# The way into the second attention of a four-layer graph network: first logits, two counts and a reload moved

## The chip, the cores and the metric

The kernel runs on one core of a Trainium2 chip. The metric is the device time of one execution in microseconds, the median of several runs. The core has TensorE (PE, matrix products), VectorE (DVE), ScalarE (ACT), GpSimd (POOL) and SyncE (SP, which here issues the DMAs). Each works through its own list of instructions in order and waits on semaphores for the others.

## The reference, cut to what matters

Four layers work on 3327 nodes with 256 features: a graph convolution, a graph convolution with a Mamba scan, a graph attention, and a last layer that holds all that is changed here. It takes two steps of diffusion and of attention with a nucleus (top-p) cut:

```
R = (S + I) / rowsum                      # S is the adjacency
Xf = X; Xa = X; Z = 0
for n in range(2):
    q = Xa @ W1.T @ W2.T;  k = Xa @ W3.T
    probs = softmax(q @ k.T)              # 3327 x 3327
    # of each row keep the largest probabilities until their sum passes 0.9
    A = probs * kept;  A = A / A.sum(-1)
    Xf = R @ Xf                           # diffusion
    Xa = A @ Xa                           # attention
    Z = Z + Xf @ U1[n].T + Xa @ U2[n].T
out = layernorm(layernorm(X + Z) + X)     # the inner one with gain g and offset b
```

"The first attention" is the pass n = 0 and "the second attention" the pass n = 1.

## The kernel before, in words

Rows are worked in 26 tiles of 128 (`nt`). For each tile of the second attention these things happen:

- **Logits.** `start(1, t, ...)` (L1655) loads the tile's query `q` by DMA, takes a buffer `e` of 128x3328 numbers, makes the generator `searches[t]` and returns the generator `scores` (L1154 and L1139). That one has four blocks; each is a pair of matmuls of 416 columns into the PSUM tile `sc`, which has one buffer, and a copy on ACT into `e`. The first attention's logits use the same function. The last of the four blocks needs the keys `kT` of tile 25.
- **Search for the cut.** `search_long` (L1421) makes ACT passes over all of `e`: an exp for a root (L1436), the exp proper with its total (L1441), then at a first cut c1 a relu sum (L1456) and a sign sum (L1458), and the same two at a second cut c2 (L1474, L1487). A sign sum is a count of the entries above the cut. Between the passes POOL computes the cuts in small steps (L1444, L1447). DVE then forms c3 (from `x` to L1497), masks each half of `e` to values below c3 (`z`, L1503), takes the top 8 of each segment of 128 (L1353), ranks the candidates in six rounds (L1364, L1366), finds the smallest kept value, drops ties (L1532) and writes the kept weights to `e` (L1540).
- **Weighted sum.** `attended` (L1318) transposes `e` on PE (L1327, 26 squares of 128), copies on ACT (`wt`) and multiplies with the features `G` (L1341), 26 products of 128x256.
- **Diffusion.** `diffused` (L1302) forms on POOL `t` (L1306 and, with `s` loaded from DRAM, L1310), multiplies 26 adjacency squares `at` with the features `F` (L1296, loads of up to five squares into three buffers), and DVE adds the two into `xf` (L1315).
- **End.** `second` (L1586 and on) does two layer norms and the store.

`first` (L1550) closes a tile of the first attention: products with U1 and U2, the sum `s` stored to DRAM (`sd`), the features of the second attention through `g` to DRAM (`gd`), and keys and queries (`store_keys`). The features go by way of DRAM since the place of `G` holds sums of feature blocks until the last pair of tiles is done. Tiles 22 and 23 are closed during the two last, single tiles, 24 and 25, and tile 25 at the end, with nothing beside it. Then `unresolved` checks the first attention's cuts, `G` is reloaded from `gd` by two DMAs (L1786), and the second attention begins.

The order of the second attention is written by hand. A loop (L1798) over i from -2 to 26 takes one step of the generators at a time: `search(i)` of the tile in work, `search(i + 1)` and `search(i + 2)` of the two that follow, the logits of tile i + 2, the weighted sum of tile i - 1 and a share of the diffusion products (`spread`). The iterations -2 to 0 are the way in: they have no weighted sum. Operations wrapped in `here` or `in_order` keep that order; a scheduler places others by their dependencies. POOL's and DVE's small steps are thus placed by the scheduler, and each engine keeps to the list that results.

Of the kernel before, what the change touches and what calls it, by code (L numbers as in the profile page):

```python
# [18 lines left out]
P = 128  # L19
D = 256  # L20
EPS = 1e-5
JH = 13
# [20 lines left out]
DL = 1  # L43
# [7 lines left out]
def gnn_kernel(ctx: ExitStack, tc: tile.TileContext, n: int, a: dict, out: bass.AP):  # L51
    nc = tc.nc
    nt = -(-n // P)
    npad = nt * P
# [122 lines left out]
    with tc.tile_pool(name="l1b", bufs=1) as wpool, tc.tile_pool(name="l1at", bufs=2) as l1at:  # L177
# [3 lines left out]
        with tc.tile_pool(name="l0", bufs=1) as pool, tc.tile_pool(name="l0w", bufs=2) as work, \  # L181
# [11 lines left out]
            for j0 in range(0, nh, J0):  # L193
# [13 lines left out]
                t1, t2, t3, t4 = (x[:, y, :HD] for x in ts)  # L207
# [4 lines left out]
            for i in range(nh):  # L212
                p1, p2, p3, p4, p5, p6, p7 = halved(atp, cmb, psum, i, top, low, ts)
                c = work.tile([P, 2, D + 1], F32, name="c", bufs=1)
                v, u = c[:, 0, HD + 1:], c[:, 1, HD + 1:]
# [9 lines left out]
                for r in range(2):  # L225
                    it = 2 * i + r
# [13 lines left out]
        with tc.tile_pool(name="l1aw", bufs=1) as cwork, tc.tile_pool(name="l1c", bufs=2) as ch, \  # L240
# [70 lines left out]
            ends = []  # L311
# [164 lines left out]
            shares = {}  # L476
# [264 lines left out]
            for k, (c, s) in enumerate(states):  # L741
# [5 lines left out]
                p = plan(c)  # L747
# [97 lines left out]
            h = prods[k % 2]  # L845
# [4 lines left out]
            for i in range(m):  # L850
                it = starts[nch - 1] // P + i
# [14 lines left out]
    half = nt // 2 * P  # L866
    nseg = npad // SEG
    with tc.tile_pool(name="l3", bufs=1) as pool, tc.tile_pool(name="l3d", bufs=1, space=DRAM) as dram:
# [245 lines left out]
        sd, gd = (dram.tile([nt, P, D], F32, name=x) for x in ("sd", "gd"))  # L1114
# [187 lines left out]
        def diffused(work, atp, psum, p, it, out, each=J3):  # L1302

            rd = rdeg[:, it:it + 1]
            t = work.tile([P, D], F32, name="t")
            nc.gpsimd.tensor_scalar(t, (Y if p else X)[:, it, :], rd, None, op0=ALU.mult)  # L1306
            if p:
                s = work.tile([P, D], F32, name="s")
                nc.sync.dma_start(s, sd[it])
                nc.gpsimd.tensor_tensor(t, t, s, op=ALU.add)  # L1310
            for acc in aggregated(atp, psum, it, Y if p else X, each):
                if acc is None:
                    yield
            d = work.tile([P, D], F32, name="xf", bufs=DL + 3)
            nc.vector.scalar_tensor_tensor(d, acc, rd, t, op0=ALU.mult, op1=ALU.add)  # L1315
            out.append(d)

# [61 lines left out]
        def t1(sm, name, w=1):  # L1379
            return sm.tile([P, w], F32, name=name)  # L1380
# [37 lines left out]
        junks = [None]  # L1418
        edge = [None]

        def search_long(work, sm, e, total, v, kept, halves=False):  # L1421

# [1 line left out]

            def t(name):
                return t1(sm, name)

            m8, neg, root = t1(sm, "m8", 8), t1(sm, "neg", 2), t("root")  # L1430
            nc.vector.max(m8, e[:, :KC])
# [19 lines left out]
            c1, nc1 = c1s[:, 0:1], c1s[:, 1:2]  # L1451
            edge[0] = nc.gpsimd.tensor_scalar(lim, total, -TOP_P, None, op0=ALU.mult)
            inverse(rc, c1)
            f1, sg, k1, m1 = t("fs1"), t("sg"), t("k1"), t("m1")
            yield
            here(nc.scalar.activation(junk, e, AF.Relu, bias=nc1, accum_out=f1))  # L1456
            yield
            here(nc.scalar.activation(junk, e, AF.Sign, bias=c1, scale=-1.0, accum_out=sg))  # L1458
            yield
            na, more, room, less, c2s = t("na"), t("more"), t("room"), t("less"), t1(sm, "c2", 2)  # L1460
            scaled(k1, sg, -0.5, npad / 2, ALU.mult, ALU.add)
# [16 lines left out]
            with tc.issue_after(second_cut.ins):  # L1478
# [5 lines left out]
                scaled(big, big, 32.0, HUGE, ALU.is_lt, ALU.mult)  # L1484
                scaled(level, f2, m1, 2.0, ALU.subtract, ALU.mult)
                scaled(level, c2, float(npad), level, ALU.mult, ALU.add)
            here(nc.scalar.activation(junk, e, AF.Sign, bias=c2, scale=-1.0, accum_out=sg))  # L1487
            yield
            x, c3 = t("x"), t("c3")
            nc.vector.reciprocal(s, s)  # L1490
# [59 lines left out]
        def first(work, psum, it, acc, f, xf, tag="pj", xa=None):  # L1550

            xa = work.tile([P, D], F32, name="h") if xa is None else xa
            nc.scalar.mul(xa, acc, f)
            yield
            pt = psum.tile([P, 4, P], F32, name=tag)
            for i, v in enumerate((xf, xa)):
                for k in range(2):
                    tensor.transpose(pt[:, 2 * i + k, :], v[:, k * P:(k + 1) * P], ident)
            xt = work.tile([P, 4, P], F32, name="xt", bufs=1)
            vector.tensor_copy(xt, pt)  # L1560
            yield
            ps = psum.tile([P, 4, P], F32, name=tag).rearrange("p (k x) d -> p k (x d)", k=2)
            for k in range(4):
                tensor.matmul(ps[:, 0, :], xt[:, k, :], (u1 if k < 2 else u2)[:, 0, k % 2, :], start=(k == 0), stop=(k == 3))
            for k in range(2):
                tensor.matmul(ps[:, 1, :], xt[:, k, :], u1[:, 1, k, :], start=(k == 0), stop=(k == 1))
            s = work.tile([P, D], F32, name="s")
            vector.tensor_add(s, ps[:, 0, :], X[:, it, :])
            nc.sync.dma_start(sd[it], s)
            nc.scalar.copy(Y[:, it, :], ps[:, 1, :])  # L1570
            yield
            pg = psum.tile([P, 4, P], F32, name=tag).rearrange("p (k x) d -> p k (x d)", k=2)
            for k in range(2):
                tensor.matmul(pg[:, 0, :], xt[:, 2 + k, :], u2[:, 1, k, :], start=(k == 0), stop=(k == 1))
            project_keys(pg[:, 1, :P], it, xt[:, 2:, :])
            g = G[:, it, :] if tag == "pj" else work.tile([P, D], F32, name="s")
            nc.scalar.copy(g, pg[:, 0, :])
            if tag != "pj":
                nc.sync.dma_start(gd[it], g)
            store_keys(work, pg[:, 1, :P], 1, it)  # L1580
            yield
# [64 lines left out]
        def both(*parts):  # L1646

            parts = list(parts)
            while parts:
                parts = [x for x in parts if next(x, parts) is not parts]  # L1650

        with tc.tile_pool(name="l3w", bufs=2) as work, tc.tile_pool(name="l3s", bufs=4) as sm:


            def start(p, t, es, searches, search):  # L1655
                if p or t:
                    q = work.tile([2 * DA, P], F32, name="q")
                    nc.sync.dma_start(q, qd[p][t])
                else:
                    q = q0  # L1660
                es[t] = work.tile([P, npad], F32, name="e", bufs=4)
                searches[t] = search(work, sm, es[t], *(x[p][:, t:t + 1] for x in (tots, vs, kepts)),
                                     **({"halves": True} if p and t == nt - 1 else {}))
                return scores(work, psum, p, q, es[t])

            with tc.tile_pool(name="l3p", bufs=2, space=PSUM) as psum, tc.tile_pool(name="l3a", bufs=1) as quads:
# [21 lines left out]
                def looks(k):  # L1688
                    for _ in range(k):
                        look()  # L1690
# [24 lines left out]
                def end_pair(i):  # L1715
                    c = next(turned[0])
                    for r in range(2):
                        it = 2 * i + r
                        f = normalizer(sm, kepts[0][:, it:it + 1], tots[0][:, it:it + 1])
                        todo[r] = [first(quads, psum, it, c[:, r, :], f, xfs[it], "tp", c[:, r, :])]  # L1720
                        next(todo[r][0])
                    ends[0] = todo[0][0]
# [16 lines left out]
                for i in range(nh - 1):  # L1739
                    stage(spread, 7, logits(2 * i + 2), ends, counts,  # L1740
                          {0: lambda: end_pair(i - 1) if i else None, 5: lambda: attend_to(i)})
                    counts = [1, 2, 2, 2, 2, 0, 0]
                    queue.append(searches[2 * i + 2])
                    values = turned[0]
                    for k in range(7):
                        next(values)
                        looks(k in (1, 2, 4, 5, 6))
                    stage(spread, 6, logits(2 * i + 3), todo[1], [2, 1, 2, 1, 2, 1], {})
                    finish()
                    queue.append(searches[2 * i + 3])  # L1750
                    for k in range(6):
                        next(values)
                        if k == 0:
                            for _ in spread:
                                pass
                        if k == 3:
                            spread = spreading(i + 2)
                        looks(k > 1)
                end_pair(nh - 2)
                todo = [x for y in todo for x in y]  # L1760
                values = attended(quads, psum, es[nt - 2], X, acc=psum.tile([P, 2, 512], F32, name="acc")[:, 0, :D])
# [2 lines left out]
                for it in (nt - 2, nt - 1):  # L1764
# [14 lines left out]
                        pass  # L1779
                    ends = first(quads, psum, it, acc, f, xfs[it], "tp", c)  # L1780
                    next(ends)
                both(ends)
                fl0 = unresolved(sm, psum, 0)
                fixed = False
            for x in (slice(0, JH), slice(JH, nt)):
                nc.sync.dma_start(G[:, x, :], gd[x].rearrange("t p d -> p t d"))  # L1786

            with tc.tile_pool(name="l3q", bufs=3, space=PSUM) as psum, tc.tile_pool(name="l3at", bufs=3) as atp, \
                    tc.tile_pool(name="l3b", bufs=2) as lone:
                es, searches, xfs = {}, {}, []
                result = iter(())
                spread = (x for j in range(nt) for x in diffused(lone, atp, psum, 1, j, xfs, 1))
                later = (nt - 2) * nt
                shares = [later * (k + 1) // (nt - 1) - later * k // (nt - 1) for k in range(nt - 1)]
                for i in range(-2, nt + 1):  # L1798
                    def search(t):
                        if 0 <= t < nt:  # L1800
                            next(searches[t])
# [3 lines left out]
                        values = attended(lone, psum, es[i - 1], G, 3, in_order(nc.scalar.copy))  # L1805
                    if i + 2 < nt:
                        logits = start(1, i + 2, es, searches, search_long)
                    share = iter(range(shares[i - 1] if 0 < i < nt else nt if -2 < i < 1 else 0))

                    def diffuse(products):  # L1810
                        for _ in range(products):
# [192 lines left out]
```

## Time and profile before

| | |
|---|---|
| runs, median (lowest to highest) | 3408.01 us (3407.56 to 3412.42) |
| profiled execution, own time | 3412.8 us |
| its span | 3411.0 us |
| PE busy | 3129.6 us, 92% |
| DVE busy | 2687.8 us, 79% |
| ACT busy | 1729.9 us, 51% |
| POOL busy | 1132.1 us, 33% |
| mean granted PE clock | 0.965 |
| last matmuls of the first attention | about 2570 us |
| first transposes of the second attention's weights | 2639.46 us |

Times of single instructions are counted from the span's start. A line of a timeline has the start, the duration, engine, line of the code, operation, output and inputs, shape and how often, and in brackets how long the engine had been idle and who released it. A line of the windows view has the stretch, its length, the busy time of PE, PE's weight loads, DVE, ACT and POOL with the number of instructions, the granted PE clock, the share of DMA time and GB/s. A matmul of 32-bit numbers shows as two records.

### The profile page before, as it was taken

Reading aid. Unit: us, or ns where it says so; the run is one execution under the profiler, and the core shown is the slowest. Engines: PE = TensorE matmul, PEld = TensorE weight load, DVE = VectorE, ACT = ScalarE, POOL = GpSimd, SP = SyncE. Lnnn points to the kernel's source line nnn. Section 1 sums busy time; section 2 is a strip of 40 time slices with the busy share of each in tenths; the row PEclk is TensorE's granted clock in tenths of the full one; section 3 lists DMA queues with packets and bytes.
Section 4 is the critical chain, followed back from the end, with each engine's and each line's share of the span. In section 5 each row is a group of like instructions: output and inputs, shape, how many; then the busy total and the mean of one; then the engine's idle time right before and its main releaser. Section 6 shows DMA issues by size and latency. Waiting matters only on the chain. (4 is left out here: it accounts for less than half of the span.)

```text
span 3411.0 us, 50267 instructions
## 1 busy us (share of the span) xinstructions
PE 3129.6 (92%) x18301; PEld 2561.4 (75%) x18301; DVE 2687.8 (79%) x5899; ACT 1729.9 (51%) x2763; POOL 1132.1 (33%) x1328
## 2 busy tenths in 40 slices
PE   8999888988888766999989999999997899999997
PEld 5999656666676555888868888888885677777776
DVE  4665268999999997877578778878863889999996
ACT  1000556767667676111133333333336888888883
POOL 0000145656665654111310000000003566666663
PEclk9999998999999888999989999999998999999999
DMA  6775334434343221544322222323213122222221
GB/s 198 249 254 190 111 99 118 113 109 113 102 122 90 67 59 42 177 139 152 111 88 79 81 72 80 87 65 88 79 49 108 40 68 67 64 63 73 72 63 36
DMA packets 206263, 344.31 MB, mean 101 GB/s; under 512 B 22222, under 2 KB 129166, under 8 KB 205870
## 3 DMA queue, kind: packets, MB, share of 16 engines
q1 hardware_dynamic: 205998, 340.92, 33.8%
q8 instruction: 148, 2.42, 0.3%
q14 instruction: 117, 0.96, 0.1%
HBM read 304.65 MB, written 36.21 MB: 100 GB/s over the span
## 5 line engine op out<-in xcount | busy, mean ns | idle before, releaser
L330 POOL TENSOR_TENSOR h<-du,row 128x2048 f32<-128x2048 f32 (+1 forms) x110 | 465.9, 4236 | 344.6 <-DVE hc L330 249.8
L330 DVE TENSOR_TENSOR_SCAN h<-dA,carry,h 128x512 f32<-128x512 f32 (+1 forms) x384 | 448.9, 1220 | 18.2 <-ACT dA L337 18.1
L337 ACT ACTIVATE dA<-t,A_log 128x512 f32<-128x512 f32 (+1 forms) x448 | 292.6, 658 | 146.9 <-DVE h L330 145.2
L1296 PE MATMUL acc<-F,at 128*128 128x256 f32 x1352 | 343.9, 383 | 3.0 <-DMA at<-in_adjT 2.1
L1341 PE MATMUL acc<-G,wt 128*128 128x256 f32 x1352 | 333.0, 388 | 6.6 <-ACT wt L1139 6.3
L1079 PE MATMUL acc<-F,at 128*128 128x257 f32 x1352 | 303.4, 381 | 0.7 <-ACT r L1023 0.7
L389 PE MATMUL cb<-F,at 128*128 128x256 f32 x1196 | 294.7, 394 | 8.3 <-ACT hn L409 3.4
L1341 PEld LDWEIGHTS acc<-G,wt 128*128 128x128 f32 x1352 | 249.1, 191 | 62.6 <-ACT wt L1139 32.7
L1146 POOL MEMSET e<- 128x1 f32 x52 | 4.9, 99 | 835.2 <-PE tp L891 770.1
L1296 PEld LDWEIGHTS acc<-F,at 128*128 128x128 f32 x1352 | 240.7, 190 | 53.2 <-issue 21.5
L1079 PEld LDWEIGHTS acc<-F,at 128*128 128x128 f32 x1352 | 253.4, 190 | 36.3 <-issue 1.0
L680 PE MATMUL y<-ident,hc 128*128 128x128 f32 x1664 | 235.5, 295 | 46.9 <-DVE hc L330 46.8
L680 PEld LDWEIGHTS y<-ident,hc 128*128 128x128 f32 x1664 | 209.2, 153 | 88.8 <-DVE hc L330 63.9
L389 PEld LDWEIGHTS cb<-F,at 128*128 128x128 f32 x1196 | 229.4, 198 | 58.5 <-issue 19.6
L330 DVE TENSOR_TENSOR hc<-h,row 128x2048 f32<-128x2048 f32 (+2 forms) x114 | 242.9, 2133 | 11.4 <-PE y L680 4.3
L891 PE MATMUL acc<-X,at 128*128 128x128 f32 (+1 forms) x988 | 173.7, 287 | 6.1 <-issue 6.1
L1263 ACT COPY wt<-tp 128x512 f32<-128x512 f32 x156 | 90.8, 589 | 166.1 <-PE tp L891 152.8
L138 PE MATMUL acc<-t,cb 128*128 128x128 f32 (+1 forms) x1014 | 168.4, 275 | 0.0
L891 PEld LDWEIGHTS acc<-X,at 128*128 128x128 f32 x988 | 142.2, 193 | 30.2 <-issue 25.3
L891 PE MATMUL acc<-G,sw 128*128 128x128 f32 x936 | 155.5, 275 | 0.0
L891 DVE MAX8 cand<-e 128x8 f32<-128x128 f32 x676 | 139.8, 277 | 5.5 <-ACT e L1160 3.8
L1160 ACT COPY e<-sc 128x832 f32<-128x832 f32 x78 | 65.9, 845 | 149.4 <-PE sc L891 149.4
(417 smaller groups left out, 7274.2 us busy)
## 6 DMA issues: line engine op xcount, KB each, us to landing
at<-in_adjT SPq DMA_DIRECT2D x54, 832.0 KB, 4.5
at<-in_adjT SPq DMA_DIRECT2D x130, 320.0 KB, 3.0
row<-bc SPq DMA_DIRECT2D x80, 512.0 KB, 5.1
at<-in_adjT SPq DMA_DIRECT2D x52, 640.0 KB, 5.5
at<-in_adjT SPq DMA_DIRECT2D x52, 576.0 KB, 4.3
at<-in_adjT SPq DMA_DIRECT2D x72, 256.0 KB, 3.2
at<-mixed SPq DMA_DIRECT2D x72, 256.0 KB, 3.6
mixed<-cb SPq DMA_DIRECT2D x26, 640.0 KB, 4.2
```

The costliest lines, as they stand in the source:

```text
L138: mm = nc.tensor.matmul(acc, w[:, j, :], x, start=(y == 0 and k % 3 == 0 and k < 6), stop=(y == nh - 1 and k in (2, 6)))
L330: return lambda *x, **k: tc.keep_in_program_order(op(*x, **k))
L337: decays.append(op(*x, **k))
L389: ten.matmul(acc, at[:, j % JC, :], X0[:, j, :], start=(j == 0), stop=(j == nt - 1))
L680: x = ten.matmul(y[:, g * P:(g + 1) * P], h[:, g, i * P:(i + 1) * P], ident, is_transpose=True, start=(first and g == 0), stop=(last and g ...
L891: return lambda *x, **k: tc.keep_in_program_order(op(*x, **k))
L1079: nc.tensor.matmul(acc, at[:, j, :], F[:, j0 + j, :], start=(j0 + j == 0), stop=(j0 + j == nt - 1))
L1146: nc.gpsimd.memset(e[:, n:], NEG)
L1160: copy(halves[:, :, c0:c0 + ws[0]], pl[:, :, :ws[0]])
L1263: nc.scalar.copy(wts[-1], pt)
L1296: nc.tensor.matmul(acc, at[:, j, :], rhs[:, j0 + j, :], start=(j0 + j == 0), stop=(j0 + j == nt - 1))
L1341: tensor.matmul(acc, wt[:, j, :], rhs[:, j0 + j, :], start=(j0 + j == 0), stop=(j0 + j == nt - 1))
```

## The change

- `search_long` gets a function `signs` for the two counts. For tile 0 (`counted`) it takes each count on DVE, as two tensor_scalar instructions over half of `e` each, with a sum and a small step behind, where the others keep ACT's sign pass.
- `start(1, 0)` is called in the first attention's end. The four blocks of tile 0's logits are interleaved with the steps of `first` for tile 25, in the first attention's PSUM pool.
- Tiles 22 to 25 write their features straight into `G`, without `gd`. The reload of `G` covers tiles 0 to 21 and stands ahead of the end of tiles 22 to 25.
- The iterations -2 and -1 of the loop are replaced by a list of pairs: a step of a search (or, with `None`, of tile 1's logits) and a number of diffusion products. In it tile 1's logits and root pass stand beside tile 0's passes. The loop now begins at 0.
- `xf` gets one more buffer (5 instead of 4).

```diff
-            d = work.tile([P, D], F32, name="xf", bufs=DL + 3)
+            d = work.tile([P, D], F32, name="xf", bufs=DL + 4)
...
-        def search_long(work, sm, e, total, v, kept, halves=False):
+        def search_long(work, sm, e, total, v, kept, halves=False, counted=False):
...
+            def signs(c):
+                ks, sg = t1(sm, "ks", 2), t("sg")
+                if counted:
+                    for h in range(2):
+                        z = lone.tile([P, half], F32, name="z", bufs=1)
+                        nc.vector.tensor_scalar(z, e[:, h * half:(h + 1) * half], c, 0.0, op0=ALU.is_gt, op1=ALU.add,
+                                                accum_out=ks[:, h:h + 1])
+                    nc.vector.tensor_add(sg, ks[:, :1], ks[:, 1:])
+                    nc.vector.tensor_scalar(sg, sg, -2.0, float(npad), op0=ALU.mult, op1=ALU.add)
+                else:
+                    here(nc.scalar.activation(junk, e, AF.Sign, bias=c, scale=-1.0, accum_out=sg))
+                return sg
...
-            here(nc.scalar.activation(junk, e, AF.Sign, bias=c1, scale=-1.0, accum_out=sg))
+            sg = signs(c1)
...
-            here(nc.scalar.activation(junk, e, AF.Sign, bias=c2, scale=-1.0, accum_out=sg))
+            sg = signs(c2)
...
-            g = G[:, it, :] if tag == "pj" else work.tile([P, D], F32, name="s")
+            direct = tag == "pj" or it >= nt - 4
+            g = G[:, it, :] if direct else work.tile([P, D], F32, name="s")
             nc.scalar.copy(g, pg[:, 0, :])
-            if tag != "pj":
+            if not direct:
                 nc.sync.dma_start(gd[it], g)
...
-                                     **({"halves": True} if p and t == nt - 1 else {}))
+                                     **({"halves": t == nt - 1, "counted": t == 0} if p else {}))
...
+                for x in (slice(0, JH), slice(JH, nt - 4)):
+                    nc.sync.dma_start(G[:, x, :], gd[x].rearrange("t p d -> p t d"))
                 end_pair(nh - 2)
...
-                both(ends)
+                es, searches = {}, {}
+                groups = start(1, 0, es, searches, search_long)
+                for _ in ends:
+                    next(groups)
+                    next(groups)
+                both(groups)
                 fl0 = unresolved(sm, psum, 0)
                 fixed = False
-            for x in (slice(0, JH), slice(JH, nt)):
-                nc.sync.dma_start(G[:, x, :], gd[x].rearrange("t p d -> p t d"))
...
-                for i in range(-2, nt + 1):
+                groups = start(1, 1, es, searches, search_long)
+                for t, products in ((0, 0), (0, 0), (None, 0), (None, 4), (0, 0), (None, 0), (None, 4),
+                                    (0, 0), (0, 0), (None, 0), (None, 4), (0, 0), (None, 0), (None, 4),
+                                    (0, 0), (1, 0), (1, 4), (0, 0), (0, 6)):
+                    next(groups if t is None else searches[t], None)
+                    for _ in range(products):
+                        next(spread)
+                for i in range(nt + 1):
...
-                    share = iter(range(shares[i - 1] if 0 < i < nt else nt if -2 < i < 1 else 0))
+                    share = iter(range(shares[i - 1] if 0 < i < nt else nt if i < 1 else 0))
```

More of the change, by code (lines that the diff above doesn't have):

```diff
@@ L1453, in search_long @@
             inverse(rc, c1)
-            f1, sg, k1, m1 = t("fs1"), t("sg"), t("k1"), t("m1")
+            f1, k1, m1 = t("fs1"), t("k1"), t("m1")
             yield
@@ L1781, in gnn_kernel @@
                     next(ends)
-                both(ends)
+                es, searches = {}, {}
[4 more added lines that the diff above has]
+                both(groups)
                 fl0 = unresolved(sm, psum, 0)
                 fixed = False
-            for x in (slice(0, JH), slice(JH, nt)):
-                nc.sync.dma_start(G[:, x, :], gd[x].rearrange("t p d -> p t d"))
             with tc.tile_pool(name="l3q", bufs=3, space=PSUM) as psum, tc.tile_pool(name="l3at", bufs=3) as atp, \
                     tc.tile_pool(name="l3b", bufs=2) as lone:
-                es, searches, xfs = {}, {}, []
+                xfs = []
                 result = iter(())
```

## The prediction

> **What bounds the kernel now.** I read the windows view first, to see where TensorE (PE) is not full. From the middle of the second attention on it is full: 50.00 of 50 us, at a granted clock of 1.00. The hole lies at that attention's start.
>
> ```profile
> 2550.00:2575.00 25.00, 20.82 (x102) 15.79 (x100) 2.79 (x9) 5.86 (x15) 1.55 (x4) 0.92 0.17 43
> 2575.00:2600.00 25.00, 22.20 (x83) 13.38 (x84) 1.08 (x2) 18.93 (x18) 4.96 (x12) 0.81 0.53 165
> 2625.00:2650.00 25.00, 15.57 (x72) 11.93 (x73) 22.38 (x65) 14.89 (x13) 11.19 (x24) 0.80 0.16 49
> 2950.00:3000.00 50.00, 50.00 (x246) 38.51 (x245) 45.56 (x136) 45.10 (x44) 32.06 (x66) 1.00 0.26 76
> ```
>
> So whatever PE loses between about 2562 and 2700 us is never caught up, and what it does not lose there comes off the end. PE's timeline shows the loss:
>
> ```profile
> 2570.64 1.48 PE L1154 MATMUL sc<-kT,q 64*128 64x416 f32 x4 [1.93 <-ACT q L907]
> 2573.12 1.76 PE L1154 MATMUL sc<-kT,q 64*128 64x416 f32 x4 [0.99 <-ACT e L1139]
> ...
> 2639.46 1.97 PE L1327 MATMUL tp<-ident,e 128*128 128x128 f32 x8 [9.09 <-DVE e L1540]
> ```
>
> The idle brackets from 2562 to 2640 us add up to 19.0 us. The longest is 9.09 us ahead of the first transposes of tile 0's weights (I call their start T0): PE has run out of products and waits for VectorE (DVE). From T0 to 2702 the brackets give 8.75 us more, mostly DVE's e again. So the start is bound by **tile 0's chain**, logits to T0. The chain of waits in this window, and the timelines of ScalarE (ACT), DVE and GpSimd (POOL), give its joints:
>
> ```profile
> 2592.13 3.06 ACT junk L1456 x2
> ...
> 2595.99 3.07 ACT junk L1458 x2
> ...
> 2604.29 3.17 ACT junk L1474 x2
> 2607.49 3.16 ACT junk L1487 x2
> ```
> ```profile
> 2581.33 3.07 ACT L1436 ACTIVATE junk<-e,neg 128x3328 bf16<-128x3328 f32 x1
> ...
> 2591.28 0.85 ACT L1139 COPY e<-sc 128x832 f32<-128x832 f32 x1 [2.24 <-PE sc L1154]
> ```
> ```profile
> 2610.76 0.27 DVE L1444 TENSOR_SCALAR x<-sg,c,level 128x1 f32<-128x1 f32 x1 [5.20 <-ACT junk L1487]
> ...
> 2612.74 1.95 DVE L1503 SCALAR_TENSOR_TENSOR z<-e,c 128x1664 f32<-128x1664 f32 x1
> ...
> 2628.70 0.16 DVE L1490 RECIPROCAL s<-s 128x1 f32<-128x1 f32 x1 [2.03 <-POOL s L1444]
> ...
> 2635.72 3.67 DVE L1540 SCALAR_TENSOR_TENSOR e<-e,v 128x3328 f32<-128x3328 f32 x1
> ```
> ```profile
> 2579.87 0.72 POOL L1310 TENSOR_TENSOR t<-t,s 128x256 f32<-128x256 f32 x1 [4.21 <-DMA s<-sd]
> ...
> 2617.83 2.57 POOL L1306 TENSOR_SCALAR t<-F,rdeg 128x256 f32<-128x256 f32 x1 [2.10 <-DVE xf L1315]
> ```
>
> The reader is to see four ACT passes of 3.2 us in series with POOL's small steps between (L1456 to L1487), tile 1's logit copies in their midst, and then a DVE stretch of 27 us.
>
> [...] The trace's 128x1664 z row takes 1.95. [...] POOL's t at L1306, usually 0.94 us, took 2.57 beside a z[...]. I take 1.95 us plus 0.08 for the accumulator read[...]. [...] the same four score records take 1.76 us around 2575 and 0.97 later.
>
> **The change, step by step**, on the time scale of the profile before. I use the order of instructions on each queue of the changed program.
>
> *Logits of tile 0.* Before, they start after all of the first attention (2570.64), with PE slow and each block of about 2.7 us (1.76 score, 0.95 wait for the copy); e is whole at 2581.25. After, block 1 stands right behind the last transposes (2563.6) and the others between the projections of tile 25. The projections wait about 0.1 us more. Block 2 runs at 2567.3. ACT's copies of tile 25 (G 0.37, kT 0.26, q 0.26) and of the blocks (0.85 each) interleave; block 4 needs tile 25's keys and block 3's copy, so it runs at 2571.5 to 2572.4; the last two copies (0.9) end at **2573.4: 7.9 us earlier**. [...] I take scores at 0.9.
>
> *Root and exp.* 2573.4 + 3.15 + copy 0.8 + 3.2 = 2580.6; POOL's c1 comes 0.45 later, 2581.05 (before 2588.8). POOL's in-order queue holds t+s, which waits for a load of s, ahead of these small steps. Before it ran at 2579.87, the load having started next to the second reload of G. After, the reload is issued before the last four tiles' stores and s should land near 2575.5: no delay. If it is as late as before, +3.3 us.
>
> *First count.* Before, c1 to c2 took 15.5 us: a 2.24 us wait for logits, copies of 2.6, passes of 3.2 and 3.2, and 5.2 on POOL (1.65 of it two large t operations). After, two DVE halves of 2.03 plus two small ones (0.4) end at 2585.5, beside ACT's relu pass (2581.4 to 2584.6); POOL's steps alone take 3.45 (tile 1's, 2624.11 to 2627.56). **c2 at 2589.0, 15.2 us earlier.**
>
> *Second count.* It ends at 2589.0 + 4.5 = 2593.5, but ACT's relu pass at c2 stands behind the rest of tile 1's copies and its root pass, which starts at 2587.95 and ends at 2591.15: relu 2594.35. On POOL, the two t operations of tile 2 now stand ahead of the two level steps, and t waits for a buffer that DVE's xf of tile 0 frees, itself queued behind the count: 2594.0 + 0.95 + 0.75 + 0.65 = 2596.4. Before, this stretch (c2 to x) took 6.5; after, 7.4. Lead 14.4. With t out of the way it would be 2595.1.
>
> *Candidates.* x to the end of 26 MAX8 is 11.5 us in both: 2607.9. Ranking to the end of e took 17.1 us with a 2.03 us wait for POOL's s of tile 1. That s now comes from ACT's passes on tile 1 (relu 2601.0, sign to 2608.2, root of tile 2 to 2611.5, POOL meanwhile to c2 2611.8, then s at 2613.9); DVE arrives at 2612.8, so the wait is 1.1. **T0 = 2607.9 + 16.2 + 0.1 = 2624.2, 15.2 us earlier** than 2639.46. ACT has finished tile 1's two signs by 2618.2, so nothing there is late for DVE's next tile.
>
> *After T0* the orders agree but for three products (3 x 0.47 = 1.4 us of PE), which lie after T0 now (75 ahead instead of 78). The DVE-bound waits of 8.75 us up to 2702 hide them. Next late is DVE's e of tile 1, as before.
>
> *At nothing:* the four copies that write G directly replace copies of equal length and drop four stores (0.33 us of SP each) and a 1.46 us wait, all beside PE's work; the reload of G has until 2626 to land; the extra xf buffer issues nothing; ACT loses two passes (6.3 us), which are the ones counted above. SP still has q and s loads ahead of adjacency loads: the q for tile 2 waits for tile 0's block 4, now 2572.4 instead of 2579.4, so those come no later.
>
> **Unknowns, both ends.** [...] Late s: 0 to +3.3. PE slow where I took it fast: 0 to +2. Hidden products: 0 to +1.4. Better order at the t operations and no wait for s: down to -2.4. So the gain is 15, from about 6 to about 20.
>
> **Rivals.** *A, the chain as worked out (0.66):* 15 us. *B, half of it (0.22):* the first logits come early, but POOL's t+s or ACT's root of tile 1 takes the place of the removed sign passes; only the 7.9 us of the logits stays, 3400. For it: 4.21 us of waiting on s and ACT at 22 of 25 us at 2600 to 2625. Against: without G's reload there is no cause for the late load. That the change does not do what it says belongs here: if the early query load or tile 25's keys held block 1, only the count would pay, about 6 to 7 us. *C, more (0.08):* PE never slows and the waits after T0 shrink too, 20 us, 3388. Against: tile 1's DVE stretch is not shortened. *D, slower (0.04):* with the hole gone, PE is granted a lower clock in the full stretch. Its place is 2725 to 3350, about 620 us of PE at 1.00: from a clock of 0.976 down the 15 us are used up; at 0.965 it is 3408 + 7 = 3415. Against: the clock row is 9 wherever PE is full; its 8s lie where PE is emptier.
>
> **The numbers.** The profiled execution took 3412.8 us (span 3411.0, 1.8 around it), 4.8 above the median of 3408.01. 3412.8 - 15 = 3397.8; on the median's scale 3393. The range 3385 to 3402 takes in A with its bounds and most of B and C. Faster by over 0.2% (6.8 us, about what a measurement can tell): A, C and most of B, 0.88; within: the rest of B, 0.08; slower: D, 0.04.
>
> **What would show it.** In the profile after: e of tile 0 whole near 2573; count halves of about 1.95 us; c2 near 2589; T0 near 2624 with an idle bracket of about 4 us; 50 of 50 later at 1.00. It is wrong if T0 moves by much more or less than the end does, if the count rows differ from 1.95, or if POOL's t+s still waits near 2580.

## The result, and the profile after

| | before | after |
|---|---|---|
| median of 7 runs each | 3411.88 us (3407.56 to 3418.32) | 3398.83 us (3394.59 to 3401.61) |
| ratio, 95% interval | | 0.9965 [0.9956, 0.9975] |
| span of the profiled execution | 3411.0 us | 3397.0 us |
| A: last transposes of the first attention | 2563.18 us | 2558.14 us |
| T0: first transposes of tile 0's weights | 2639.46 us | 2621.31 us |
| T0 - A | 76.3 us | 63.2 us |
| end - A | 847.8 us | 838.9 us |

The change makes the kernel 0.35% faster: 0.0035 of 3411.88 is 11.9 us, with an interval of 8.5 to 15.0. A is a mark of mine: the last `tp<-ident,sw` row on PE, which belongs to tile 25 in the first attention. Of the change, only the early reload and the direct writes of tiles 22 and 23 work before it, yet it came 5.0 us sooner in this profile. Over all profiles of this study A lies between 2553.6 and 2564.8 us, and e12 (below), which has neither of the two, has it at 2557.45. So the 5.0 of the 14.0 us between the spans are no more than executions differ among themselves, and **end - A, 8.9 us shorter, is the part of this profile that lies behind the change's place**. It is 3 us less than the runs show, but inside their interval. All stages are compared by their distance from A from here on.

The windows view after, for the four stretches shown of before (stretch, length, then busy time of PE, PE's loads, DVE, ACT and POOL, PE clock, DMA share, GB/s):

```profile
2550.00:2575.00 25.00, 20.12 (x97) 14.29 (x97) 2.74 (x7) 13.99 (x20) 4.84 (x9) 0.96 0.21 69
2575.00:2600.00 25.00, 24.53 (x104) 15.96 (x103) 16.43 (x38) 19.84 (x18) 10.56 (x28) 0.97 0.37 108
2625.00:2650.00 25.00, 22.19 (x108) 17.14 (x105) 22.13 (x68) 21.16 (x22) 11.38 (x26) 0.96 0.20 56
2950.00:3000.00 50.00, 50.00 (x245) 37.19 (x244) 45.85 (x140) 42.67 (x44) 31.50 (x57) 1.00 0.21 60
```

PE is full again later, at a clock of 1.00, as before. In the stretch at 2575 it is now busy for 24.53 us at 0.97 instead of 22.20 at 0.81, and DVE has work there (16.43 instead of 1.08 us): the counts.

The joints of tile 0's chain, from ACT's and then DVE's timeline after (start, duration, engine, line, operation, operands, and in brackets the idle time before it and who ended it):

```profile
2568.53 3.07 ACT L1449 ACTIVATE junk<-e,neg 128x3328 bf16<-128x3328 f32 x1
...
2584.11 0.91 ACT L1139 COPY e<-sc 128x416 f32<-128x416 f32 x2 [2.30 <-PE sc L1154]
2585.05 3.07 ACT L1449 ACTIVATE junk<-e,neg 128x3328 bf16<-128x3328 f32 x1
...
2588.30 3.07 ACT L1487 ACTIVATE junk<-e,c 128x3328 bf16<-128x3328 f32 x1
```
```profile
2576.04 1.95 DVE L1435 TENSOR_SCALAR_CACHE_REDUCE z<-e,c 128x1664 f32<-128x1664 f32 x1 [2.98 <-POOL c L1457]
...
2592.29 0.27 DVE L1457 TENSOR_SCALAR x<-sg,c,level 128x1 f32<-128x1 f32 x1 [3.18 <-POOL level L1457]
...
2610.39 0.16 DVE L1503 RECIPROCAL s<-s 128x1 f32<-128x1 f32 x1 [2.12 <-POOL s L1457]
...
2617.56 3.69 DVE L1553 SCALAR_TENSOR_TENSOR e<-e,v 128x3328 f32<-128x3328 f32 x1
```

The first L1449 row is tile 0's root pass; it starts at A + 10.4, and the first count half at A + 17.9. The second L1449 row is tile 1's root pass. It stands between tile 0's second cut (c2 is there by 2584.12, when its count starts) and tile 0's second relu pass (L1487), and tile 1's last logit copies ahead of it waited 2.30 us for PE. That puts L1487 at 2588.30, and DVE's x waits 3.18 us for what POOL makes of it.

PE's timeline after, at its first products, at T0 and at tile 1's transposes:

```profile
2572.17 3.86 PE L1296 MATMUL acc<-F,at 128*128 128x256 f32 x10 [2.70 <-issue]
...
2577.04 2.43 PE L1296 MATMUL acc<-F,at 128*128 128x256 f32 x10
...
2621.31 1.31 PE L1327 MATMUL tp<-ident,e 128*128 128x128 f32 x10 [2.04 <-DVE e L1553]
...
2647.75 1.69 PE L1327 MATMUL tp<-ident,e 128*128 128x128 f32 x8 [2.81 <-DVE e L1553]
2649.23 1.92 PE L1296 MATMUL acc<-F,at 128*128 128x256 f32 x4
```

The bracket at T0 fell from 9.09 to 2.04 us. Ten records of products (five products) took 3.86 us behind the first wait, where the ten that follow take 2.43 us; four records took 1.92 us behind the 2.81 us wait, where the same row took 1.03 in the kernel before. Up to 62.5 us past T0, PE also waited 1.69 and 1.54 us for ACT's copies `wt` and 4.28 us for tile 2's e.

After T0 something is given back: tile 2's e is whole 60.5 us after T0 instead of 56.7, and end - T0 is 775.7 instead of 771.5 us. Two DVE rows carry it, and a POOL row that one of them leads to:

```profile
2652.26 0.48 DVE L1600 SCALAR_TENSOR_TENSOR h<-acc,f,xf 128x256 f32<-128x256 f32 x1 [4.26 <-PE acc L1341]
...
2678.08 0.16 DVE L1503 RECIPROCAL s<-s 128x1 f32<-128x1 f32 x1 [1.65 <-POOL s L1457]
```
```profile
2671.61 0.94 POOL L1306 TENSOR_SCALAR t<-F,rdeg 128x256 f32<-128x256 f32 x1 [5.00 <-DVE xf L1315]
```

The same place in the kernel before, PE and then DVE:

```profile
2665.60 1.06 PE L1327 MATMUL tp<-ident,e 128*128 128x128 f32 x8 [1.19 <-DVE e L1540]
2666.51 1.03 PE L1296 MATMUL acc<-F,at 128*128 128x256 f32 x4
```
```profile
2666.47 0.16 DVE L1490 RECIPROCAL s<-s 128x1 f32<-128x1 f32 x1 [1.01 <-POOL s L1444]
...
2668.44 0.48 DVE L1586 SCALAR_TENSOR_TENSOR h<-acc,f,xf 128x256 f32<-128x256 f32 x1 [1.55 <-PE acc L1341]
...
2692.37 0.15 DVE L1490 RECIPROCAL s<-s 128x1 f32<-128x1 f32 x1
```

Behind tile 1's e, DVE waited 2.56 us in two steps before and 4.26 us after, 1.7 us more. The wait of 1.65 us for POOL's s ahead of tile 2's e did not exist before. Together they are 3.4 of the 3.8 us by which tile 2's e is later.

### The profile page after: what moved, and what is told of

The parts are those of the page before. It is cut to its first block, busy times and chain, and to the rows that moved or that the text cites. A ratio compares the mean times of both kernels' runs of the same rounds, so it can differ in the third digit from the quotient of the medians.

```text
span 3397.0 us, 50257 instructions
## 1 busy us (share of the span) xinstructions
PE 3123.9 (92%) x18301; PEld 2562.3 (75%) x18301; DVE 2697.8 (79%) x5911; ACT 1723.8 (51%) x2759; POOL 1125.4 (33%) x1328
## 5 line engine op out<-in xcount | busy, mean ns | idle before, releaser
L1296 PEld LDWEIGHTS acc<-F,at 128*128 128x128 f32 x1352 | 241.8, 191 | 57.2 <-issue 24.3
L1440 ACT ACTIVATE junk<-e,c 128x3328 bf16<-128x3328 f32 x50 | 154.1, 3082 | 0.0
```

What stands on the lines that cost most here:

```text
L1296: nc.tensor.matmul(acc, at[:, j, :], rhs[:, j0 + j, :], start=(j0 + j == 0), stop=(j0 + j == nt - 1))
L1440: here(nc.scalar.activation(junk, e, AF.Sign, bias=c, scale=-1.0, accum_out=sg))
```

## The experiments

Each kernel was run beside the kernel before on the same chip: e1 to e4 on one, e5 to e8 on a second, e9 to e11 on a third, e12 on a fourth. "PE idle" is the length less PE's busy time in the windows view: first from A to 66 us past T0, then from A to the end.

| | median us | ratio to before, 95% | T0 - A | end - A | PE idle, start | PE idle, all |
|---|---|---|---|---|---|---|
| before | 3411.88 | | 76.3 | 847.8 | 27.6 | 49.8 |
| after | 3398.83 | 0.9965 [0.9956, 0.9975] | 63.2 | 838.9 | 20.8 | 44.1 |
| e1 the changed kernel again | 3399.05 | 0.9967 [0.9954, 0.9980] | 63.3 | 838.7 | 18.8 | 42.0 |
| e2 signs on ACT | 3399.04 | 0.9964 [0.9951, 0.9977] | 66.0 | 838.2 | 20.0 | 42.9 |
| e3 logits late | 3401.47 | 0.9972 [0.9962, 0.9983] | 65.6 | 841.3 | 24.3 | 47.6 |
| e4 reread late | 3399.74 | 0.9961 [0.9944, 0.9977] | 64.6 | 837.9 | 19.5 | 41.6 |
| e5 old order, the rest kept | 3395.33 | 0.9955 [0.9939, 0.9971] | 63.4 | 835.1 | 16.9 | 39.6 |
| e6 nine products in the list's last pair | 3395.58 | 0.9957 [0.9940, 0.9973] | 62.7 | 835.9 | 12.6 | 38.8 |
| e7 third t buffer | 3399.24 | 0.9968 [0.9956, 0.9981] | 62.2 | 838.7 | 18.8 | 42.7 |
| e8 relu first | 3391.38 | 0.9946 [0.9930, 0.9962] | 58.0 | 832.1 | 14.3 | 37.3 |
| e9 logits alone | 3400.97 | 0.9977 [0.9970, 0.9984] | 70.6 | 841.7 | 24.7 | 47.2 |
| e10 logits and reread | 3405.46 | 0.9988 [0.9982, 0.9995] | 72.3 | 845.3 | 26.4 | 49.2 |
| e11 relu first, twelve products in the last pair | 3399.51 | 0.9974 [0.9962, 0.9987] | 60.6 | 840.8 | 15.7 | 43.1 |
| e12 counts alone | 3405.73 | 0.9985 [0.9972, 0.9998] | 70.2 | 844.2 | 25.1 | 47.6 |

PE's busy time from A to the end (end - A less the last column) is 794 to 798 us in all of them. So **the end is PE's work, nearly the same in all, plus PE's idle time, wherever that lies**. "Nearly" counts where effects are small: of the 8.9 us between before and after, 5.8 are idle time and 3.2 are busy time (slow rows, such as the 3.86 us for 2.43 above, count as busy). T0 alone does not give the end: e2 has its T0 2.8 us later than the changed kernel and an end no later.

The profiles of the changed kernel, of e1 and of e7, which have one order, agree within 0.2 us in end - A, though T0 - A differs by up to 1.1 us. The edits also shift how many diffusion products the traces show ahead of T0: 75 in the changed kernel, 78 in e2, 70 in e4, 74 in e5 and e6, 68 in e8. A difference is therefore that of an edit with what the scheduler made of it.

**First round: one part undone at a time.** e1 is the changed kernel. The edits of the others:

```diff
# e2
-    **({"halves": t == nt - 1, "counted": t == 0} if p else {})
+    **({"halves": t == nt - 1, "counted": False} if p else {})
# e3
-                for _ in ends:
-                    next(groups)
-                    next(groups)
+                both(ends)
                 both(groups)
# e4
-            direct = tag == "pj" or it >= nt - 4
+            direct = tag == "pj"
...            # and both rereads of G, over all tiles, behind the first attention
```

> The changed kernel itself, once more. In its first profile the instructions ahead of the last transposes of tile 25 (which the change does not touch) came 5.0 us earlier than in the profile of before; from those transposes to the first transposes of tile 0's weights (T0) it took 63.2 us against 76.3. Theory 'noise ahead': the 5 us are run-to-run variation of the earlier layers; here the transposes of tile 25 lie anywhere within 2558 +- 6 us, the stretch to T0 is again 63.2 +- 0.3 and from T0 to the end 775.7 +- 1.5, and the ratio of times stays at 0.9965 +- 0.001. Rival 'placement': the change makes earlier layers faster; then the transposes stand at 2558 +- 1 again.

> Tile 0's two counts go back to ScalarE's sign passes; all else stays. Theory 'the counts pay because they free ScalarE': two passes of 3.2 us return to its queue, tile 1's passes come 6.4 us later, and VectorE, which waits in tile 0's ranking for a number of tile 1, follows: stretch to T0 63.2 -> 69 to 70 us, time +5 to +6.5 us (+0.15 to 0.19%). Rival 'the logits alone pay': relu and sign fit beside other work and T0 moves by less than 1 us.

> Tile 0's logits are made after tile 25 is closed, no longer between its projections (still ahead of the check of the first attention's cuts); all else stays. Theory: tile 0's root pass, now 10.4 us after the last transposes of tile 25, starts 5 to 8 us later and T0 with it: stretch 63.2 -> 68 to 71 us, time +5 to +8 us. Rival 'ScalarE's queue decides': tile 0's search is held up later in any case, and T0 moves by less than 3 us.

> The features go through DRAM for all tiles again and the second reload stands after the first attention, as before; logits, counts and order of passes stay. Theory: s for GpSimd and the first adjacency squares land behind 1.7 MB of features: GpSimd's t + s 4 to 5 us later, the first cut 1 to 2 us later, and T0 with it: stretch 64.5 to 66.5 us, time +1 to +3.5 us. Rival 'hidden anyway': no change of T0 (within 0.5 us).

Measured: e1 repeated the stretches from A to T0 and to the end. Its A of 2558.53 us suits its rival too; against the rival speaks that A lies at 2564.78 in e6 and at 2557.45 in e12. Each part undone costs 2.4 us at the most, in end - A and in the medians, and by the runs none of the three differs from e1 beyond the intervals. e2 missed widely: T0 came 2.8 us later instead of 6 to 7, and the end was no later, for end - T0 was 772.2 instead of 775.7 us. e3 missed too, as its rival said; it undoes only a part of the logits' lead, since tile 0's root pass starts at A + 13.1, against A + 15.3 in e12, where the logits stand in their old place, and A + 10.4 in the changed kernel. In e4 T0 came 1.4 us later, as expected, but the end did not follow. Two readings were left: the list of the way in brings the rest, or the parts stand in for each other, so that taking one away shows little.

**Second round: the list, and what lies after T0.**

```diff
# e5: the list goes, the loop begins at -2 again
-                groups = start(1, 1, es, searches, search_long)
-                for t, products in ((0, 0), (0, 0), (None, 0), (None, 4), (0, 0), (None, 0), (None, 4), ...
-                for i in range(nt + 1):
+                for i in range(-2, nt + 1):
# e6
-                                    (0, 0), (1, 0), (1, 4), (0, 0), (0, 6)):
+                                    (0, 0), (1, 0), (1, 4), (0, 0), (0, 9)):
# e7, at L1305 and L1601
-            t = work.tile([P, D], F32, name="t")
+            t = work.tile([P, D], F32, name="t", bufs=3)
# e8: tile 0's second relu ahead of tile 1's root pass
-                                    (0, 0), (1, 0), (1, 4), (0, 0), (0, 6)):
+                                    (0, 0), (1, 0), (0, 0), (1, 4), (0, 6)):
```

> Undone: the list of the way in. The loop starts at -2 again, so that tile 1's logits and passes stand where they stood before the change, behind tile 0's; the early logits, the counts on DVE and the early reload stay. Theory (what counts is TensorE's idle time from the first attention's last transposes to 66 us past the second's first ones: 27.5 us before, 20.5 and 18.3 in two profiles of the changed kernel): tile 1 comes late again, the idle time rises to 23 to 26 us and the end, counted from the first attention's last transposes, is 4 to 6 us later than the 838.8 of the changed kernel. Rival (the list only changes who waits; the early logits and the reload bring all of it): within 1.5 us of the changed kernel. Rival from the prediction's sum (the lead at the first transposes decides): with tile 0's chain free of tile 1's passes the first transposes come 1 to 3 us earlier than 63.2, and the end as much earlier.

> Three more products on TensorE just ahead of the first transposes (the list's last pair asks for 9 instead of 6), so that 111 instead of 104 stand ahead of tile 2's. Nothing else is moved ahead of the first transposes. Theory (idle time of TensorE decides, and the lead at the first transposes is given back because too few products lie ahead of tile 2): the first transposes keep 63.2 within 1 us after the first attention's last ones, the waits of TensorE for tiles 1 and 2 shrink from 10.3 us to 7 to 9, and the end comes 1.5 to 4 us earlier. Rival (after the first transposes VectorE's chain decides, and products only fill its waits): end within 1 us. Rival (the three products delay tile 0): first transposes 1.4 us later and the end 1 to 2 us later.

> One more buffer for the features' step t on POOL (3 instead of 2), nothing else: the order of TensorE's and VectorE's instructions is that of the changed kernel. In the changed kernel POOL's t at 2671.61 waits 5.00 us for VectorE's xf, and VectorE's reciprocal at 2678.08 then 1.65 us for POOL. Theory (that wait is a part of what is lost after the first transposes): the 1.65 us goes, the third tile's logits are whole 1.5 to 2 us earlier, and the end with them. Rival (VectorE waits for the products next, whoever released it first): the waits move to h and the end stays within 0.8 us.

> In the list tile 0's second ReLU pass goes ahead of tile 1's root pass (3.07 us each on ACT), the products ahead of the first transposes fall from 75 to 68. Theory (tile 1's root pass, which starts late because TensorE is late with tile 1's scores, stands in tile 0's chain): x of tile 0 comes 2.5 to 3.3 us earlier, the first transposes 2 to 3 us earlier than 63.2 after the first attention's last ones; since seven products are lost ahead of them, tile 1 then waits longer for products or root pass and half or more of that is given back: end 0 to 1.5 us earlier. Rival (lead decides): end 2 to 3 us earlier. Rival (idle time decides): idle time up by 2 to 4 us and the end as much later.

*e5* went against all three theories: without the list the end is 3.8 us **earlier** by the profile, at the same T0 - A. The intervals of e5 and of the changed kernel overlap. But e7, which keeps the list and ended as the changed kernel did, ran beside e5 on the same chip, and in 63 of the 66 pairs of one run of each e5's is the shorter; the medians differ by 3.9 us. So with the other three parts in place the list costs time. Without the counts it is the other way round: e2 has the list and e10 (third round) has not, and their intervals lie apart, at 12.3 and 4.1 us of gain. PE's row for tile 1 in e5:

```profile
2650.28 1.06 PE L1327 MATMUL tp<-ident,e 128*128 128x128 f32 x8 [2.38 <-DVE e L1553]
```

After 2.38 us of waiting the eight transposes took 1.06 us (1.69 in the changed kernel after 2.81), DVE's h waited 2.15 us instead of 4.26, and the wait for POOL's s did not come up. That is 2.1 + 1.65 = 3.8 us, nearly all of the difference in tile 2's e (56.6 against 60.5 us past T0). What in the list brings these waits about is not shown. Nor does a wait of a given length always come with a slow row behind it. Tile 1 of e4, then tile 2 of e8 and tile 2 of e6:

```profile
2653.31 1.45 PE L1327 MATMUL tp<-ident,e 128*128 128x128 f32 x8 [2.04 <-DVE e L1553]
```
```profile
2673.93 1.94 PE L1327 MATMUL tp<-ident,e 128*128 128x128 f32 x8 [2.46 <-DVE e L1553]
```
```profile
2686.30 1.06 PE L1327 MATMUL tp<-ident,e 128*128 128x128 f32 x8 [2.47 <-DVE e L1553]
```

Tile 1 of e8 (shown below) took 1.06 us after 2.05. So a bracket's length alone does not decide it; what does is not shown.

*e6* ended as its theory said, 3.0 us earlier by end - A and with no delay at T0, though its six runs reach from below those of e7 into their upper half, so that the runs do not settle it. The trace has the products elsewhere than expected: 74 stand ahead of T0, one fewer than in the changed kernel, and 111 instead of 104 ahead of tile 2's transposes. There PE's two waits for ACT's `wt` are gone, its wait for tile 2's e is 2.47 instead of 4.28 us, and DVE no longer waits for POOL's s; h of tile 1 still waits 4.26 us. PE's waits in the 62.5 us from T0, without the one at T0, fall from 10.3 to 5.3 us. The lowest idle time at the start (12.6 us) is partly given back later: 5.0 us of idle follow up to the last 350 us, where the changed kernel has 2.9. *e7* refutes its theory: the reciprocal's wait fell from 1.65 to 0.37 us, but another of 1.10 us came up at tile 1's reciprocal, and the end stayed within 0.2 us.

*e8* has the largest gain of all: its six runs (3388.80 to 3395.23) lie below all eleven of e7 (3396.16 to 3407.76), which ran beside it and differs from the changed kernel by a buffer that brought nothing. ACT's, DVE's and PE's rows:

```profile
2583.69 3.08 ACT L1487 ACTIVATE junk<-e,c 128x3328 bf16<-128x3328 f32 x1
...
2586.90 3.07 ACT L1449 ACTIVATE junk<-e,neg 128x3328 bf16<-128x3328 f32 x1
```
```profile
2587.68 0.27 DVE L1457 TENSOR_SCALAR x<-sg,c,level 128x1 f32<-128x1 f32 x1 [0.44 <-POOL level L1457]
```
```profile
2643.63 1.06 PE L1327 MATMUL tp<-ident,e 128*128 128x128 f32 x8 [2.05 <-DVE e L1553]
```

L1487 now stands ahead of L1449, x waits 0.44 instead of 3.18 us and comes 3.3 us earlier (A + 30.8 instead of A + 34.2), and the wait of 2.12 us for tile 1's s is gone from tile 0's chain. T0 is 5.2 us earlier and the end 6.8 us, more than any of the three theories said, so nothing of it was given back. The 3.3 us at x are the pass moved; e8 also has 68 instead of 75 products ahead of T0, and what that adds was not taken apart.

**Third round: parts added one by one to the kernel before,** in the old order, and e8 with more products.

```diff
# e9: e5 with e2's and e4's edits     e10: e5 with e2's edit
# e11: e8 with
-                                    (0, 0), (1, 0), (0, 0), (1, 4), (0, 6)):
+                                    (0, 0), (1, 0), (0, 0), (1, 4), (0, 12)):
# e12: the kernel before with `signs` and
-    **({"halves": True} if p and t == nt - 1 else {})
+    **({"halves": t == nt - 1, "counted": t == 0} if p else {})
```

> The first part of the change alone: tile 0's logits in the first attention's end. Old order of the second attention (loop from -2, tile 1 behind tile 0), signs of tile 0 on ACT, all tiles of gd reread after the first attention. Counted from the first attention's last transposes, the end was 847.8 us before, 838.8 in the changed kernel and 835.1 in the old order with the three other parts (e5). Theory (the parts overlap: each undone alone cost 2.4 us or nothing, the logits 2.4): the logits alone bring 5 to 8 us, end at 840 to 843. Rival (the logits are what the 2.4 us of e3 say, and the counts bring the rest once the list is away): 845 to 846.

> The early logits and the early reread of the features, in the old order, with tile 0's signs on ACT. From e5 it differs by the counts alone, from e9 by the reread alone. Theory (the counts shorten tile 0's chain by 2 x 1.0 us and free 6.2 us of ACT for tile 1; in the old order nothing of tile 1 waits for VectorE instead): end 1.5 to 3.5 us later than e5's 835.1. Rival (as e2 showed in the new order, the counts bring nothing): within 1 us of e5. The reread: TensorE's wait for its features' blocks (10.0 us in e4) is gone against e9, and the end 0 to 2 us earlier.

> e8 (tile 0's second ReLU ahead of tile 1's root pass) with the list's last pair at 12 products instead of 6, so that 67, 89 and 111 products stand ahead of the first transposes of tiles 0, 1 and 2 instead of 68, 87 and 104. Theory (e6's gain of 3 us came from TensorE's waits for tiles 1 and 2, which e8 still has: 0.85 to 2.46 us each, 6.9 in all): first transposes within 1 us of e8's 58.0, end 1.5 to 3.5 us earlier than e8's 832.1. Rival (e8 has taken the same time away already): end within 1 us of e8.

> The kernel before with one part of the change: tile 0's two sign passes as count halves on VectorE. Logits, reread and order as before. Theory (ACT is what tile 0 and tile 1 share: without the two passes of 3.07 us tile 0's second ReLU and tile 1's passes come sooner, worth 10.2 us between e10 and e5): the counts alone bring 7 to 10 us, the end 838 to 841 us after the first attention's last transposes instead of 847.8, the first transposes 7 to 9 us earlier than 76.3. Rival (only tile 0's own chain gets shorter, by two times 3.07 + 0.18 - 3.97): 2 to 3 us. Rival (the counts are worth something only with the early logits): within 1.5 us of the kernel before.

*e9*: the early logits alone bring 7.8 us by the ratio (5.5 to 10.2), as its theory said, though their delay in e3 cost only 2.4. *e10*: the early reread on top did not help but cost 3.6 us in end - A, and 4.5 us between the medians of 22 runs each, taken side by side; the ends of the two intervals just overlap, and e10's run is the longer in 372 of 484 pairs. PE's wait ahead of its first products did fall from 5.80 to 2.15 us, but DVE's wait for tile 1's s grew from 2.25 to 4.41. In the list's order (e4) the reread made no difference. Why it costs in the one order is open.

*e10 to e5* adds only the counts: end - A falls by 10.2 us, far more than expected. ACT's timelines show how, first e10, then e5:

```profile
2582.21 3.09 ACT L1440 ACTIVATE junk<-e,c 128x3328 bf16<-128x3328 f32 x1
...
2585.42 3.07 ACT L1449 ACTIVATE junk<-e,neg 128x3328 bf16<-128x3328 f32 x1
...
2589.00 3.07 ACT L1487 ACTIVATE junk<-e,c 128x3328 bf16<-128x3328 f32 x1 [0.42 <-POOL c L1457]
...
2592.20 3.07 ACT L1440 ACTIVATE junk<-e,c 128x3328 bf16<-128x3328 f32 x1
```
```profile
2587.39 3.07 ACT L1449 ACTIVATE junk<-e,neg 128x3328 bf16<-128x3328 f32 x1
...
2590.64 3.07 ACT L1487 ACTIVATE junk<-e,c 128x3328 bf16<-128x3328 f32 x1
```

The two L1440 passes are gone. Counted from A, L1487 starts 3.5 us sooner (30.2 against 33.7) and x comes 3.7 us sooner; since ACT also gets to tile 1 sooner, DVE's wait of 4.41 us for tile 1's s is gone too. That makes 8.1 of the 8.9 us that T0 gains.

*e12*: the counts alone bring 5.1 us (0.7 to 9.5) by the ratio, between theory and rival, and 3.6 us by end - A. PE's first score blocks in e12, where the code ahead is that of before:

```profile
2566.85 0.97 PE L1154 MATMUL sc<-kT,q 64*128 64x416 f32 x4 [1.00 <-ACT e L1139]
2568.77 0.97 PE L1154 MATMUL sc<-kT,q 64*128 64x416 f32 x4 [0.95 <-ACT e L1139]
```

In the profile of before these rows took 1.76 us. Tile 0's root pass starts at A + 15.3 in e12 and at A + 18.2 before. So 2.9 of the 76.3 us of T0 - A before go with PE's slow rows in that execution; how often they fall there two profiles cannot tell.

*e11* failed: the end is 8.7 us later than in e8. DVE waits 2.77 us for tile 1's s again, T0 is 2.6 us later, PE's bracket there is 5.73 us, and 4.2 us of idle time stand in the last 200 to 60 us, where e8 has 0.9. That the products taken earlier are missing there is likely, but no run shows it.

By the ratios, then: logits 7.8 us, counts 5.1, logits with reread 4.1, the same with the list 12.3, logits with reread and counts 15.3, these three with the list 11.9 and with the list in e8's order 18.4. The counts and the list stand in for each other: on top of logits and reread each brings 8 to 11 us alone, and both together no more than one.

## Why the prediction was right, and where not

It forecast 15 us, 3393.0, and the measurement gives 11.9: inside the range, on the predicted side. By end - A the gain is 8.9 us, so the 15 were too many by 3 to 6 us. A sign that the prediction itself named for being wrong came up: T0 moved by 13.1 us against A, the end by 8.9.

- **Logits.** Predicted 7.9 us; root pass at A + 10.3 predicted, A + 10.4 measured. But 2.9 of the 7.9 were PE's slow rows in the one profile of before, which the prediction showed (1.76 against 0.97) and yet counted as the change's. That the sum came out is in this part luck.
- **First count.** Four halves of 1.95 us were expected, 1.95 with 0.08 for the read were measured; POOL's small steps beside the second count (2584.29 to 2585.85) took 0.19 to 0.31 us each, the same steps before 0.19 to 0.34. c2 at A + 25.8 predicted, A + 26.0 measured. The estimate, drawn from the z row of before (1.95 us for 128x1664, 0.08 for its read), held.
- **Second count.** The mis-sized term. Tile 1's root pass ahead of the relu was seen, but its start was put at 2587.95 on the scale of before, A + 24.8; it was A + 26.9. The rows point to the unknown "PE slow where I took it fast", taken at 0: PE's first products waited 2.70 us and ran at 3.86 for 2.43, so tile 1's scores came late. No run took this alone; the rows only agree with it. x was due at A + 33.2 and came at A + 34.2, although POOL's t was not in the way.
- **Ranking.** The wait for tile 1's s was 2.12 us instead of 1.1. With the second count this makes T0's lead 13.1 instead of 15.2 us.
- **After T0.** The step that failed: "the orders agree but for three products ... hide them". 4.2 us were lost there, 1.7 of them where DVE waited for tile 1's products, behind PE's slow rows after a 2.81 us wait (1.69 us for 1.06, 1.92 for 1.03), and 1.65 at POOL's s. In e5 neither came up, and end - T0 is 771.7 us, where before had 771.5. Taking most of the second away alone brought nothing (e7). The prediction also misread the waits that were to hide the products: of its 8.75 us, 3.63 are DVE's e and 5.12 ACT's `wt`. In the changed kernel the waits up to the same row did not shrink but grew, to 11.2 us against 8.75, so that nothing was hidden; seven more products ahead of tile 2's transposes made them shorter (e6).
- **The reread at nothing.** Right for the changed kernel (e4); as part of the old order it cost (e10).
- The profiled spans differ by 14.0 us, close to the 15, but only because 5.0 us of variation ahead of A fill what was lost after T0. That is luck.
- Rival D is out: 50.00 of 50 us at 1.00. Rival B cannot be put aside. Its 8 us are almost as near to 11.9 as the 15 are, and nearer to the 8.9 of end - A. ACT's root of tile 1 did come into tile 0's chain, as B feared: about 1 us more than the prediction had allowed for, and 3.3 us at x against an order without it (e8). And in the changed kernel the counts bring nothing at the end (e2). Against B stands that delaying the logits costs 2.4 us at the most (e3), and that without the list the counts are worth 10.2 us (e10 to e5).

The prediction treated the four parts as one chain whose terms add. The runs show that in the old order the counts work through ACT's queue (3.7 us by x and 4.4 by tile 1's s), and that the list does not add to them. They also show a pass of tile 1 that delays tile 0: its root pass stands ahead of tile 0's second relu in the old order too (e5's rows), where before the change it filled a wait of ACT for c2; once the counts made c2 early, it stood in the way.

## What to carry to other kernels

Where an engine is full later on, price a change to its ramp by that engine's idle time over the whole ramp and tail, not by the lead at one milestone: here 2.8 us at T0 were worth nothing in one case (e2), and 5.2 us went with 6.8 in another (e8). When several parts act on one chain, what one is worth depends on which others are there: the counts brought nothing at the end where the list was, and 10.2 us where it was not. Undo a part and add it alone before calling it useless. In an in-order queue, ask of each pass of the next tile whether its input can be late, and if so put the leading tile's pass first: in e8 this brought x 3.3 us earlier.

## What the hardware showed that was not expected

At the start of the second attention, after bracketed waits of 1.84 to 2.70 us with smaller waits around them, ten records of products on PE took 3.86 to 4.47 us instead of 2.43 (in the changed kernel, e5, e8, e10 and e11), and after waits of one length, 2.04 and 2.05 us, eight transposes took 1.45 us in one execution (e4) and 1.06 in another (e8). And the same score rows ran at 1.76 us in one execution (before), with no single wait above 1.93 us in the 10 us ahead of them, and at 0.97 in another (e12) with the same code ahead: a row's duration from a stretch with a clock of 0.81 is not a property of the row.
